# A decoder kernel whose constants and first transfers become operations of its graph, with causal maxima taken as negated minima

## The chip, the cores and the metric

The kernel runs on one core of a Trainium2 chip as one program. The metric is the device time of one execution in microseconds (us). The core has a TensorE (PE: matmuls, with weight loads listed apart as PEld), VectorE (DVE), ScalarE (ACT), GpSimd (POOL) and SyncE (SP), which here only issues transfers. Each engine works through its own stream of instructions in order, and waits on semaphores where it needs what another engine or a transfer made.

## What is computed

The reference is a decoder of four layers on `x` of 4 batches x 256 tokens x 128 features, in float32, with a context `ctx_768` of 4 x 512 x 96 and a mask on the context. Every stage adds to `x`:

```python
x = x + _L0_attn_ref(_layernorm(x), W, b)                    # one head of 128
x = x + _L0_xattn_ref(_layernorm(x), ctx_768, Wq, ..., q_down, q_up, ..., Wk_ipa, Wv_ipa)
...
x = x + _L2_attn_ref(_layernorm(x), Q, K, V, O)              # 16 heads of 64, causal
...
x = x + _L3_attn_ref(_layernorm(x), Wq, Wk, Wv)              # one head of 64, causal
x = x + _L3_xattn_ref(_layernorm(x), ctx_768, ...)
x = x + _L3_ffn_ref(_layernorm(x), ...)                      # 6 layers of local attention and a gated FFN
```

Two pieces matter for the change. In the first cross attention each of the four weights gets a low-rank addition, `W + down @ up * (alpha / 32)`, and the last 4 of the 512 context tokens are image tokens with weights of their own. In the two causal attentions the scores of later tokens are masked, then comes a softmax: maximum of a row, exponential of the difference, sum, division.

## The kernel before, in words

The kernel keeps `x` in four tiles, one for each batch, of 128 partitions x 2 x 128. It is written as a graph: each `op` names an entry of the table `NET` (or `LOCAL` for the last stage) with its engine, an estimated duration and a due time, and lists the buffers that it reads and writes. `Flow.order` (a list scheduler that runs when the kernel is built) sorts all operations of all stages: among the operations that could start first on an engine it takes the one that is due first, and it hands out buffers of an arena (`TILES` says how many of a kind there are). The stages are interleaved by batch in the order of `ORDER`. So what stands next to what on an engine comes from the due times. Where the scheduler sees TensorE wait, it puts filler transposes of the identity matrix in front (`keep`, L412, of tile `ident`): work without a use. In the program of before, TensorE starts with 34 such transposes (`WARM`), and 284 more stand at other places.

What the scheduler does not order in before is the set-up. `Decoder.prepare` (L82 to L130) and `Net.prepare` (L1055 to L1073) and `Net.run` (L1709 to L1723) issue it ahead of the graph:

- POOL makes the identity (`masks.py`), `neghalf`, `ones`, the float32 causal mask (L108, L112), three bfloat16 masks (L126, L128), zeroed tiles for later stages (L1062 to L1072: four of 256 columns, two of 1040, two of 576, and two of 65 ones) and the `pick` tile of the third cross attention (L1712, L1720).
- SP issues the four loads of `x` (L94) and two of the mask (L1715); ACT issues `cols` (the biases and scales by column), `rows` (six bias rows on all partitions) and four context tiles `ctxT` (L82, L97, L100).

Only then comes the graph. Its first operations are, for batch 0 of the first attention: layer norm (`n_stats` on DVE, L440 and L441; `n_eps` on DVE, L445; `n_root`, a power of -0.5, on POOL, L446; `n_scale` on DVE, L456), a turn on TensorE and its copy on ACT (L412, L417), then `h_qk`, `h_v`, `h_scores`, the softmax and `h_weigh`. Its weight `a0_w` is fetched by SP (L426) as an operation of the graph. The first cross attention needs `low_rank` (L819 to L865): eight fetches (for q, k, v and o one of `up`, 32 x 1024, and one of `down`, at most 32 x 128), four scalings by alpha / 32 (`l_scale`, L832), products (`l_mm`) and additions to the weights (`l_add`, L850, L863). Then `image_keys` fetches two weights into the same kind of buffer (`x4`, four of them) and multiplies them with the image tokens: 16 matmuls with only 16 columns each (`i_kv`). A transfer on SP waits for the eighth transfer ahead of it to have landed, and for its buffer to be free.

A causal maximum is one DVE instruction for each block of scores, which adds the mask, writes the sum and keeps the row's maximum; a second instruction for each pair of blocks turns the sign (L548, L777), because the exponential on ACT (L557, L781) takes the negated maximum as its bias:

```python
nc.vector.tensor_tensor_reduce(
    cols(lo, hi), ps2.t[:, lo:hi], d.causal[:, t, : hi - lo], 1.0, -3.0e38, ALU.add, ALU.max,
    one(nmx, t),
)
...
nc.vector.tensor_scalar_mul(nmx.t[:, 2 * e : 2 * e + 2], nmx.t[:, 2 * e : 2 * e + 2], -1.0)
```

The second layer's causal attention has 16 heads in pairs: 4 batches x 8 pairs x 2 heads gives 64 such `c_max` operations, with 2 blocks each. The last layer's has one head: 4 `h_max`.

Of the kernel before, what the change touches and what calls it, by code (L numbers as in the profile page):

```python
# [30 lines left out]
P = 128  # L31
# [17 lines left out]
    ("x0_qal", 1), ("x0_kal", 1), ("x0_val", 1), ("x0_oal", 1), ("desc", 8),  # L49
# [17 lines left out]
class Decoder:  # L67
# [17 lines left out]
    def prepare(self):  # L85
# [3 lines left out]
        self.cols = c.tile([P, NCOL], F32, tag="cols", name="cols")  # L89
        self.rows = self.early.tile([P, NROW], F32, tag="rows", name="rows")  # L90
        self.x = []
        for b in range(B):
            xb = c.tile([P, 2, D], F32, tag=f"x{b}", name=f"x{b}")
            nc.sync.dma_start(out=xb, in_=self.a["x"][b].rearrange("(t p) d -> p t d", p=P))  # L94
            self.x.append(xb)
        self.load(self.cols, "cols", nc.scalar)
        nc.scalar.dma_start(out=self.rows, in_=self.a["rows"].partition_broadcast(P))  # L97
        self.ctxT = self.early.tile([CD, B, NCTX], F32, tag="ctxT", name="ctxT")
        for b in range(B):
            nc.scalar.dma_start(out=self.ctxT[:, b, :], in_=self.a["ctxT"][b])  # L100
# [4 lines left out]

        def mask(name, keeps):
            m = self.early.tile([P, 2, S], F32, tag=name, name=name)
            nc.gpsimd.memset(m, 0.0)  # L108
            for t in range(2):
                for base, q, k in keeps(t):  # L110

                    nc.gpsimd.affine_select(  # L112
                        out=m[:, t, :], in_=m[:, t, :], compare_op=ALU.is_ge, fill=NEG,
                        base=base + q * t * P, pattern=[[k, S]], channel_multiplier=q,
                    )
            return m

        self.causal = mask("causal", lambda t: [(0, 1, -1)])

        self.ident16 = self.early.tile([P, P], BF16, tag="ident16", name="ident16")  # L120
        nc.vector.tensor_copy(self.ident16, self.ident)
        self.causal16 = self.early.tile([P, P], BF16, tag="causal16", name="causal16")
        self.band16 = self.early.tile([P, 2 * P], BF16, tag="band16", name="band16")
        for m, lo, k, q in ((self.causal16, 0, -1, 1), (self.band16, 0, -1, 1), (self.band16, P, 1, -1)):
            m = m[:, lo : lo + P]
            nc.gpsimd.memset(m, 0.0)  # L126

            nc.gpsimd.affine_select(  # L128
                out=m, in_=m, compare_op=ALU.is_ge, fill=-(2.0**100), base=0, pattern=[[k, P]],
                channel_multiplier=q,  # L130
            )
# [11 lines left out]
class Flow:  # L143
# [22 lines left out]
    SETTLED = 9.0  # L166
# [179 lines left out]
class Net:  # L346
# [72 lines left out]
    def fetch(self, kind, *parts):  # L419
# [3 lines left out]
        def dma():  # L423
            for name, lo, hi, rows, view in parts:
                out = w.t[rows if isinstance(rows, slice) else slice(rows), lo:hi]
                self.nc.sync.dma_start(out=out if view is None else view(out), in_=self.a[name])  # L426

        self.op("fetch", dma, [], [w])
# [63 lines left out]
    def biased(self, b, row, reads=()):  # L492
# [3 lines left out]
            x, x, row()[:, None, :].to_broadcast([P, 2, D])), [self.x[b], *reads], [self.x[b]])  # L496


    def one_head(self, b, w, rows, scale, biased, causal):
# [40 lines left out]
        def most():  # L540
            if causal:
                for t in range(2):
                    cut = slice(t * S, t * S + nk[t])
                    nc.vector.tensor_tensor_reduce(
                        pr.t[:, cut], sc.t[:, cut], d.causal[:, t, : nk[t]], 1.0, -3.0e38, ALU.add, ALU.max,
                        sums.t[:, t : t + 1],
                    )
                nc.vector.tensor_scalar_mul(nmx.t[:, :2], sums.t[:, :2], -1.0)  # L548
# [5 lines left out]
        def exps():  # L554
            for t in range(2):
# [3 lines left out]
                    accum_out=sums.t[:, 2 + t : 3 + t],  # L559
# [3 lines left out]
        self.op("h_max", most, [sc], [nmx, pr] if causal else [nmx], [sums, pr])  # L563
# [28 lines left out]
    def pair_weights(self, names, rows):  # L592
        view = lambda x: x.rearrange("p (g m) -> p g m", m=D)
        return {
            m: self.fetch("w4", (name, 0, 1024, rows if m in "kv" else P, view if m == "o" else None))
            for m, name in zip("qkvo", names)
# [35 lines left out]
    def cross_wide(self, stage, w, bias, image=None):  # L632
# [4 lines left out]
        for b in range(B):  # L637
# [3 lines left out]
            v, vmade, vt = self.pair_values(b, w, lambda c, b=b: d.ctxT[:, b, c * P : (c + 1) * P], [], 4)  # L641
# [14 lines left out]
    def cross_pair(self, b, g, w, xT, v, vmade, vt, oT, n, image):  # L656
# [3 lines left out]
        self.op("p_k", lambda: self.mm(pk.t[:, :n], w["k"].t[:CD, cut], d.ctxT[:, b, :n]), [w["k"]], [pk], [kT])  # L660
# [83 lines left out]
    def causal_pair(self, b, g, w, xT, v, vmade, vt, oT):  # L744
# [21 lines left out]
        for e in range(2):  # L766
# [4 lines left out]
            def masked(ps2=ps2, cols=cols, one=one, e=e):  # L771
                for t, lo, hi in tiles:
                    nc.vector.tensor_tensor_reduce(
                        cols(lo, hi), ps2.t[:, lo:hi], d.causal[:, t, : hi - lo], 1.0, -3.0e38, ALU.add, ALU.max,
                        one(nmx, t),
                    )
                nc.vector.tensor_scalar_mul(nmx.t[:, 2 * e : 2 * e + 2], nmx.t[:, 2 * e : 2 * e + 2], -1.0)  # L777

            def exps(cols=cols, one=one):
                for t, lo, hi in tiles:  # L780
                    nc.scalar.activation(  # L781
                        cols(lo, hi), cols(lo, hi), AF.Exp, bias=one(nmx, t), accum_out=one(sums, t)
# [6 lines left out]
            self.op("c_max", masked, [ps2], [prob], [p, nmx])  # L789
# [29 lines left out]
    def low_rank(self, w):  # L819

        nc, d = self.nc, self.d
        parts = {}
        for i, (m, rows) in enumerate((("q", D), ("k", CD), ("v", CD), ("o", RANK))):

            r = slice(RANK * i, RANK * (i + 1))
            low, high = ("down", "up") if m != "o" else ("up", "down")
            n = rows if m != "o" else D
            big = self.fetch("x4", (f"x0_{m}{high}", 0, 1024, r, None))
            small = self.fetch("e2", (f"x0_{m}{low}", 0, n, r, None))

            def scale(m=m, small=small, n=n, r=r):
                nc.vector.tensor_scalar(  # L832
                    small.t[r, :n], small.t[r, :n], d.col(f"x0_{m}al")[r], 1.0 / RANK, ALU.mult, ALU.mult,
                )

            self.op("l_scale", scale, [small], [small])
# [1872 lines left out]
```

## Time and profile before

| quantity | value |
|---|---|
| median of 3 runs | 2117.17 us (2116.97 to 2117.47) |
| the profiled execution's own time | 2120.44 us |
| its span, first to last instruction | 2118.5 us |
| mean granted TensorE clock | 0.986 |
| TensorE busy | 2050.2 us, 97% of the span |
| VectorE busy | 1638.8 us, 77% |
| ScalarE busy | 1179.3 us, 56% |
| GpSimd busy | 993.1 us, 47% |
| moved by DMA | 71.21 MB, mean 34 GB/s |

The profile page gives busy times, a chain of work that ended last, groups of instructions and DMA issues. The trace behind it can also be asked for a stretch of time: instructions in order, what each engine waited for, busy time and granted clock. "L412" is a line of the kernel. A line such as `PE bank L412 <- DVE arena L456: 8.5, 4, 4.4` says that TensorE, on its instruction of L412, was idle for 8.5 us in 4 waits, of which the longest was 4.4 us, and that an instruction of L456 on DVE ended them. TensorE's busy time includes the fillers, and a matmul counts as busy at half clock too.

### The profile page before, as it was taken

The page shows a single profiled execution, that of the slowest core. Times are in us where ns is not written, and L with a number is a line of the kernel's source. Part 1 is how long each engine was busy: PE and PEld are TensorE (multiplying, and loading weights), DVE is VectorE, ACT ScalarE, POOL GpSimd, SP SyncE. Part 2 cuts the span into 40 slices and gives each one's busy share as a digit, 9 for nine tenths or more (in the row PEclk, how much of TensorE's full clock was granted, in tenths as well). Part 3 has the DMA queues.
Part 4 walks back from the last instruction along what each step waited for, and adds up shares of the span by engine and source line. Part 5 has one row for each costly group of instructions (what it writes and reads, how often), then busy time and mean ns, then how long its engine had stood idle before and what let it go on. Part 6 is the DMA issues. An engine that isn't in the chain of part 4 may idle for free.

```text
span 2118.5 us, 59911 instructions
## 1 busy us (share of the span) xinstructions
PE 2050.2 (97%) x24498; PEld 1373.6 (65%) x24499; DVE 1638.8 (77%) x4352; ACT 1179.3 (56%) x2668; POOL 993.1 (47%) x1155
## 2 busy tenths in 40 slices
PE   8999999999999998899999999999999999999998
PEld 6666675776675666666665666666656666666666
DVE  4767777788787668988887688789788797797882
ACT  2654727344536677566565565556556465556553
POOL 3334415231312245445364357557567465575660
PEclk8999999999999999999999999999999999999999
DMA  5000020111020000100000102112121021211101
GB/s 155 1 1 2 1 70 1 32 40 55 2 76 2 9 2 5 56 3 1 1 1 1 51 13 70 42 31 74 42 72 52 25 70 42 71 46 42 29 23 32
DMA packets 33425, 71.21 MB, mean 34 GB/s; under 512 B 5688, under 2 KB 17984, under 8 KB 33152
## 3 DMA queue, kind: packets, MB, share of 16 engines
q1 hardware_dynamic: 20320, 50.29, 8.0%
q10 hardware_dynamic: 12832, 17.09, 2.5%
q8 instruction: 194, 3.18, 0.6%
q14 instruction: 79, 0.65, 0.1%
HBM read 41.68 MB, written 0.52 MB: 20 GB/s over the span
## 4 chain that ended last, share of the span: by engine, by line
PE 68%; DVE 22%; POOL 5%; issue 3%; ACT 2%; DMA 1%; POOLq 0%; SPq 0%; ACTq 0%; DVEq 0%
PE bank L409 39%; PE bank L1828 17%; PE bank L412 9%; PE bank L2044 2%; DVE arena L1982 2%; DVE arena L1992 2%; DVE arena L1997 2%; POOL arena L2034 2%; DVE arena L1603 1%; POOL arena L1996 1%; POOL arena L2077 1%; PE bank L2118 1%; DVE arena L2085 1%; DVE arena L417 1%; DVE arena L2087 1%
## 5 line engine op out<-in xcount | busy, mean ns | idle before, releaser
L409 PE MATMUL bank<-arena 128*64 128x256 f32 (+11 forms) x6824 | 857.5, 393 | 10.5 <-ACT arena L1525 3.6
L409 PEld LDWEIGHTS bank<-arena 128*128 128x128 f32 (+4 forms) x6824 | 532.6, 165 | 276.8 <-issue 100.0
L1828 PE MATMUL bank<-arena 64*64 64x32 f32 (+3 forms) x13584 | 651.7, 251 | 6.4 <-issue 2.6
L1828 PEld LDWEIGHTS bank<-arena 64*64 64x64 f32 (+2 forms) x13584 | 387.4, 127 | 209.3 <-issue 115.9
L417 ACT COPY arena<-bank 128x512 f32<-128x512 f32 (+4 forms) x586 | 269.6, 489 | 286.1 <-PE bank L409 199.9
L1996 POOL TENSOR_TENSOR arena<-arena 128x1024 f32<-128x1024 f32 x96 | 226.7, 2364 | 124.1 <-PE bank L1828 63.4
L691 POOL TENSOR_SCALAR arena<-arena 128x508 f32<-128x508 f32 (+1 forms) x256 | 176.8, 697 | 209.2 <-DVE arena L688 184.1
L412 PEld LDWEIGHTS bank<-ident,arena 128*128 128x128 f32 x1757 | 196.6, 141 | 116.2 <-issue 47.3
L412 PE MATMUL bank<-ident,arena 128*128 128x128 f32 x1757 | 253.5, 280 | 18.3 <-DVE arena L456 8.5
L686 ACT ACTIVATE arena<-bank,arena 128x508 f32<-128x508 f32 (+1 forms) x256 | 175.3, 691 | 78.6 <-DVE arena L684 36.6
L2034 POOL TENSOR_TENSOR arena<-arena 128x1024 f32<-128x1024 f32 x96 | 180.9, 1905 | 71.8 <-DVE arena L2018 71.8
L1990 ACT ACTIVATE arena<-bank 128x512 f32<-128x512 f32 x192 | 113.9, 601 | 133.2 <-PE bank L1828 105.7
L684 DVE TENSOR_REDUCE arena<-bank 128x1 f32<-128x508 f32 (+1 forms) x256 | 164.2, 676 | 18.6 <-PE bank L409 18.4
L1002 ACT ACTIVATE arena<-bank 128x512 f32<-128x512 f32 (+1 forms) x256 | 124.6, 582 | 63.9 <-PE bank L409 62.4
L417 DVE COPY arena<-bank 128x512 f32<-128x512 f32 (+1 forms) x196 | 125.8, 667 | 42.9 <-PE bank L412 27.7
L1992 DVE TENSOR_TENSOR arena<-bank,arena 128x512 f32<-128x512 f32 x192 | 127.5, 683 | 38.0 <-ACT arena L1990 36.4
L2077 POOL TENSOR_TENSOR arena<-arena 128x1024 f32<-128x1024 f32 x48 | 91.4, 1904 | 108.5 <-ACT arena L2050 62.7
L1982 DVE TENSOR_TENSOR arena<-bank,arena 128x256 f32<-128x256 f32 x384 | 138.4, 411 | 3.1 <-ACT arena L1990 2.7
L979 DVE TENSOR_REDUCE arena<-bank 128x1 f32<-128x512 f32 (+2 forms) x256 | 116.7, 513 | 21.5 <-PE bank L409 21.1
L2050 ACT COPY arena<-bank 128x512 f32<-128x512 f32 x192 | 103.3, 601 | 28.8 <-PE bank L2044 28.7
L1997 DVE TENSOR_REDUCE arena<-arena 128x16 f32<-128x1024 f32 x96 | 114.3, 1201 | 0.0
L2044 PEld LDWEIGHTS bank<-ident,arena 128*128 128x128 f32 x768 | 87.0, 142 | 42.0 <-POOL arena L2034 21.8
(230 smaller groups left out, 2460.7 us busy)
## 6 DMA issues: line engine op xcount, KB each, us to landing
arena<-arena SPq DMA_DIRECT2D x48, 384.0 KB, 3.9
arena<-in_f_w SPq DMA_DIRECT2D x24, 512.0 KB, 3.5
arena<-in_f_wqkv ACTq DMA_DIRECT2D x18, 512.0 KB, 7.0
arena<-arena SPq DMA_DIRECT2D x48, 128.0 KB, 2.3
arena<-in_f_wo ACTq DMA_DIRECT2D x6, 512.0 KB, 4.0
arena<-in_f_w ACTq DMA_DIRECT2D x6, 341.0 KB, 3.9
arena<-in_f_w ACTq DMA_DIRECT2D x6, 192.0 KB, 6.2
arena<-in_x_wq SPq DMA_DIRECT2D x2, 512.0 KB
```

Of the source, the lines that this page charges most:

```text
L409: self.nc.tensor.matmul(out, lhsT, rhs, start=start, stop=stop)
L412: self.nc.tensor.transpose(out, in_, self.d.ident)
L417: return self.op(name, lambda: copy(out(), in_()), reads, writes, holds)
L684: self.op("p_max", lambda ps=ps, one=one: nc.vector.tensor_reduce(one(nmx), ps.t[:, :n], AX.X, ALU.max, negate=True), [ps], [most], [nmx])
L686: self.op("p_exp", lambda ps=ps, one=one, cols=cols: nc.scalar.activation(cols(), ps.t[:, :n], AF.Exp, bias=one(nmx), accum_out=one(sums)) ...
L691: nc.gpsimd.tensor_scalar(cols(), cols(), one(sums), 1.0, ALU.mult, ALU.mult)
L1828: self.nc.tensor.matmul(out, lhsT, rhs, start=start, stop=stop)
L1982: nc.vector.tensor_mul(heads(tmp.t[:, cut])[:, :, lo : lo + 32], heads(ps.t)[:, :, 32 - lo : 64 - lo], spread(1, lo, lo + 32),)
L1992: op("cosine", lambda cut=cut, ps=ps: nc.vector.tensor_mul(heads(out.t[:, cut]), heads(ps.t), spread(0, 0, 64)), [ps, w["tab"]], [out])
L1996: op("rotary", lambda: nc.gpsimd.tensor_add(out.t, out.t, tmp.t), [out, tmp], [out])
L1997: op("norms", lambda: nc.vector.tensor_reduce(ss.t[:, at : at + 16], heads(sq.t), AX.X, ALU.add), [sq], [ss])
L2034: nc.gpsimd.tensor_mul(heads(out.t), heads(out.t), rs.t[:, at : at + 16, None].to_broadcast([P, 16, 64]))
```

## The change

The first transfers and the constants become operations of the graph with names, durations and due times of their own (`load_*`, `k_*`); only the identity, `neghalf`, `ones` and the load of `cols` stay ahead of it. All other loads are issued by SP, in the order of their due times; `rows` and `ctxT` leave ACT's queue. The eight low-rank fetches become two, `x0_ups` (128 x 1024) and `x0_downs` (128 x 128), with one scaling for all four. `WARM` falls from 34 to 20. In the causal maxima, the scale of the masked sum is -1.0 and the reduction a minimum, so that the result is the negated maximum; the instruction that turned the sign goes, and the exponential gets the scale -1.0. All due times of `NET` and `LOCAL` are set anew, most by a few units.

```diff
-        self.load(self.cols, "cols", nc.scalar)
-        nc.scalar.dma_start(out=self.rows, in_=self.a["rows"].partition_broadcast(P))
...
-        for b in range(B):
-            nc.scalar.dma_start(out=self.ctxT[:, b, :], in_=self.a["ctxT"][b])
...
+    def load_context(self, b):
+        self.nc.sync.dma_start(out=self.ctxT[:, b, :], in_=self.a["ctxT"][b])
...
                     nc.vector.tensor_tensor_reduce(
-                        cols(lo, hi), ps2.t[:, lo:hi], d.causal[:, t, : hi - lo], 1.0, -3.0e38, ALU.add, ALU.max,
+                        cols(lo, hi), ps2.t[:, lo:hi], d.causal[:, t, : hi - lo], -1.0, 3.0e38, ALU.add, ALU.min,
                         one(nmx, t),
                     )
-                nc.vector.tensor_scalar_mul(nmx.t[:, 2 * e : 2 * e + 2], nmx.t[:, 2 * e : 2 * e + 2], -1.0)
...
-                        cols(lo, hi), cols(lo, hi), AF.Exp, bias=one(nmx, t), accum_out=one(sums, t)
+                        cols(lo, hi), cols(lo, hi), AF.Exp, bias=one(nmx, t), scale=-1.0, accum_out=one(sums, t)
...
+        big = self.fetch("x4", ("x0_ups", 0, 1024, P, None), name="load_ups")
+        small = self.fetch("h", ("x0_downs", 0, D, P, None), name="load_low")
+        self.op("l_scale", lambda: nc.vector.tensor_scalar(
+            small.t[:, :D], small.t[:, :D], d.col("x0_al"), 1.0 / RANK, ALU.mult, ALU.mult), [small], [small])
...
+        begun = Buffer()
+        for b in range(B):
+            self.op("load_x", lambda b=b: d.load_x(b), [], [self.x[b], begun])
+            self.op("load_ctx" if b else "load_ctx0", lambda b=b: d.load_context(b), [], [self.context[b]])
+        self.op("load_rows", d.load_rows, [], [self.rows])
+        self.op("k_causal", d.fill_causal, [begun], [self.causal])
+        self.op("k_ident", lambda: nc.vector.tensor_copy(d.ident16, d.ident), [begun], [self.masks])
+        self.op("k_masks", d.fill_masks, [begun], [self.masks])
...
+        self.op("k_pads", empty, [begun], [b for bufs in pads.values() for b in bufs])
+        self.op("k_values", values, [begun], [self.fixed("vs", self.vss) for _ in self.vss])
+        self.op("k_image", image, [begun], [self.fixed("vb", self.vbs) for _ in self.vbs])
+        self.op("k_pick", pick, [begun], [self.pick])
+        self.op("load_mask", mask, [], [self.pick])
...
+    "load_a": ("SP", 0.8, -900.0),
+    "load_x": ("SP", 0.55, -800.0),
+    "load_low": ("SP", 0.3, -700.0),
+    "load_ups": ("SP", 2.05, -690.0),
+    "load_wk": ("SP", 1.55, -600.0),
+    "load_ctx0": ("SP", 0.8, -540.0),
+    "load_wv": ("SP", 1.55, -500.0),
+    "load_wq": ("SP", 2.05, -400.0),
+    "load_ctx": ("SP", 0.8, -300.0),
+    "load_rows": ("SP", 1.55, -250.0),
+    "load_image": ("SP", 1.55, -200.0),
+    "load_wo": ("SP", 2.05, -150.0),
+    "load_mask": ("SP", 0.9, 30.0),
+    "k_causal": ("POOL", 1.4, 43.74),
+    "k_ident": ("DVE", 0.2, -2.50),
+    "k_masks": ("POOL", 1.7, 7.01),
+    "k_pads": ("POOL", 1.3, -0.06),
+    "k_values": ("POOL", 2.4, 1.19),
+    "k_image": ("POOL", 1.3, 2.10),
+    "k_pick": ("POOL", 3.1, 37.01),
...
-WARM = 34
+WARM = 20
```

The order that the scheduler makes of it can be read off the built programs, instruction by instruction, without any time. On SP the loads stand as in the table above: `a0_w`, the four of `x`, `x0_downs`, `x0_ups`, the weight of k, the first context tile, the weights of v and q, three context tiles, `rows`, the two image weights, the weight of o, the mask. On POOL the first `n_root` stands right behind the identity, ahead of all zeroed tiles, masks and `pick`. On TensorE the 14,099 instructions other than fillers are the same in both programs, and only their places differ, in these stretches (times are those of the profile before): the start up to 81.3 us; small swaps between 169 and 370 us and between 697 and 719 us; 1131 to 1142 us; 1234 to 1354 us, where the last stage begins; and 2002 to 2083 us, before its end. Fillers: 318 before (34 at the start, 45 more in its first 27 us, 18 between 1284 and 1292 us, 8 at 2078 us), 269 after (20 at the start, none until 441 us, 36 between 1270 and 1287 us, none at 2078 us); the others stand where they stood.

## The prediction

> **What bounds the kernel now.** I read the page first (busy times, chain), then TensorE's waits, then the first 50 us instruction by instruction, since most of the change lies there.
>
> ```profile
> PE 2050.2 (97%) x24498; PEld 1373.6 (65%) x24499; DVE 1638.8 (77%) x4352; ACT 1179.3 (56%) x2668; POOL 993.1 (47%) x1155
> PE 68%; DVE 22%; POOL 5%; issue 3%; ACT 2%; DMA 1%; POOLq 0%; SPq 0%; ACTq 0%; DVEq 0%
> ```
>
> TensorE is busy 97% of the span and makes 68% of the chain. So a microsecond counts only where TensorE waits, runs fillers, or runs at half clock. The waits of the first 30 us:
>
> ```profile
> PE bank L412 <- DVE arena L456: 2.9, 2, 2.5
> PE bank L409 <- DVE arena L832: 2.3, 2, 1.4
> PE bank L412 <- POOL ident masks.py:199: 1.6, 1, 1.6
> PE bank L409 <- ACT arena L417: 0.5, 1, 0.5
> ```
>
> What ends them is in the timeline, from layer norm 0 to the low-rank products:
>
> ```profile
> 4.48 4.02 DVE L445 TENSOR_SCALAR arena<-arena 128x2 f32<-128x2 f32 x1
> ...
> 4.86 1.89 POOL L1067 MEMSET arena<- 128x1040 f32 x2
> ...
> 7.93 0.55 POOL L1712 MEMSET pick<- 128x512 bf16 x1
> ...
> 8.58 0.72 POOL L446 TENSOR_TENSOR arena<-arena,neghalf 128x2 f32<-128x2 f32 x1
> ...
> 9.34 1.34 DVE L456 TENSOR_SCALAR arena<-x,arena 128x128 f32<-128x128 f32 x2 [0.78 <-POOL arena L446]
> ...
> 19.70 0.86 DVE L832 TENSOR_SCALAR arena<-arena,cols 32x128 f32<-32x128 f32 x3 [3.28 <-DMA arena<-in_x_qdown]
> ```
>
> Two delays are to be seen. `n_eps` takes 4.02 us, though its like takes 0.14 at 26.49: it ends at 8.50, when POOL's unbroken run of memsets ends (8.48). And the small `qdown`, last in SP's queue, lands at 19.68, so that `l_mm` starts at 20.03. The third loss is the clock, in the table of stretches (columns: time, PE, PEld, DVE, ACT, POOL, clock, DMA share, GB/s):
>
> ```profile
> 27.15:81.30 54.15, 54.15 (x272) 34.15 (x274) 32.81 (x96) 28.42 (x70) 17.92 (x52) 0.91 0.14 50
> 28.00:40.00 12.00, 12.00 (x50) 9.59 (x49) 3.30 (x10) 1.39 (x4) 2.18 (x8) 0.57 0.56 197
> ```
>
> TensorE is granted 0.57 between 28 and 40 us, that is half from 29.6 to 39.85, although it counts as busy: it runs 16-column products there.
>
> **The start, part by part.** The built programs have the same work on TensorE in the same order from 81.3 us on (but for the stretches below), so I compare the time from the first `h_qk` (11.53) to that point: 69.8 us. In it: waits 1.42 + 0.85 = 2.3; 45 fillers at about 0.12 = 5.4; half clock 10.24 x 0.5 = 5.1 and, from 12.5 to 16.0 over some 2.5 us of work, 1.2. Proper work: 69.8 - 2.3 - 5.4 - 6.3 = **55.8 us**. Now the same four terms after.
>
> *When `h_qk` starts.* `a0_w` (192 KB) is ahead of `x0` on SP, one issue of 0.5 us: statistics begin at 4.0 instead of 3.54. They take 0.94 to `n_eps`, this 0.17 (POOL is idle now), `n_root` 0.72, with gaps 5.95. Then `n_scale` meets the moved memsets. Row: at 9.34 two scales took 1.34 beside POOL's selects of 0.63, one in each gap between two of them, which wait for each other. In the new order the zeroed tiles run without a wait for 1.01 + 0.98 us, then comes a 65-column memset that waits for the one ahead: first gap 8.0, second 9.1. With the 0.85 from scale to `h_qk` as before: **10.0**. Bounds: no blocking, 7.2; blocked to the selects of `k_masks`, 11.6. The Trainium skill, page "SBUF — State Buffer", section "SBUF: two separate sides", speaks against this cost: the pair of ports that DVE and GpSimd share is locked for one instruction, so an instruction would wait for the memset under way only. By it `n_eps` would have waited 0.33 us, where the row shows 4.02; by the page `h_qk` would start near 7.6, by the row at 10.0.
>
> *Waits of TensorE after that.* Loads: between 2 and 18 us before, DMA moved 263 GB/s on average, most of it from SP alone. Summed in the new order from 2 us: weight of k 1.76 MB, 8.7 us; of v 2.35 MB, 10.9; of q 2.87 MB, 12.9; second image weight 4.64 MB, 19.6. `l_scale` and the first `l_mm` need 1.36 MB, 7.2. None is late for its first use (`l_mm` near 11, `i_kv` near 22). On DVE the six `l_add` at 0.6 stand in one row with `h_qkout` (0.9) and `h_max` (0.6): 5.1 us from 11.2 on, so the values, which need the last `l_add` of v, start near 16 to 17. TensorE has about 12 us of work from 10.0 to `i_kv`; I take waits of **3 us** (bounds 1 and 6). Queued behind an `l_add` that waits for a weight would be `h_max` and `h_recip`; the sums above leave 2 to 3 us.
>
> *Clock.* 20 starting transposes end near 5.8 instead of 7.5, then TensorE idles until 9: I expect half clock from about 9 to 12.5 or 16 and again for one record of 3.41 us around `i_kv` (its 32 passes take 0.107 each at full, 0.213 at half clock). **4.5 us** lost (bounds 1.5 and 10). The Trainium skill, page "TensorE: Matmul & The Clock Gate", section "What's actually happening", speaks against taking fillers out: an idle window of about 3.4 us halves the clock. The records here have that length too, but the half clock at 29.6 came while TensorE was fed: being fed alone did not keep it.
>
> Sum: 10.0 + 55.8 + 3 + 4.5 = 73.3 against 81.3: **-8.0 us** (bounds 65.5, -15.8; 83.4, +2.1). The 18 transfers, at 0.3 to 0.5 us of issue each, are SP's alone now; SP waits for the eighth before, with over 1 MB under way. ACT loses five issues and is free for its table at 1.3 instead of 8.56; that was hidden already.
>
> **Causal maxima.** 64 + 4 instructions go, of the group
>
> ```profile
> L777 DVE TENSOR_SCALAR arena<-arena x64: 168/169/1161, 661.7 to 916.0; 128x2 f32<-128x2 f32 x64
> ```
>
> whose mean is 0.216 us: 13.9 us of DVE. The number of other instructions stays, so the minimum and the scale of -1 cost what the maximum (0.28 and 0.41) and the exponential (0.40) cost. On the path: between 661 and 925 us TensorE waited 4.1 us in 9 waits for the shares behind this chain, each shorter by 0.2, so **-2.0**. Bounds: all of it on the path, -14.8; nothing, and a clock record of 3.41 us more by a shifted phase, +1.7. Its cover is TensorE's own work; where DVE is fullest,
>
> ```profile
> 795.00:901.00 106.00, 93.86 (x622) 67.15 (x620) 96.87 (x356) 65.60 (x210) 50.13 (x75) 0.95 0.10 31
> ```
>
> half of the 64 stand, and 12 us of TensorE's idle time, mostly behind the latent softmax and not behind `c_max`: what is late next.
>
> **Later orders.** From 1234 to 1354 us other attention heads go first and the first projections of the last stage later; 36 fillers replace 18: +18 x 0.11 = 2.0 if all are on the path, nothing if they fill waits that are there anyway (5.8 us). I take **+1.0**; bounds -5.8 (waits gone) and +5.6 (36 at half clock less 18). Before the end 8 fillers go and the order differs: **-0.5**; bounds -3.2 and +3.2 (the waits in that stretch).
>
> **Sum.** -8.0 - 2.0 + 1.0 - 0.5 = -9.5. Span 2118.5 - 9.5 = 2109.0; with the 1.9 around it 2110.9. The profiled execution is 3.3 above the median, so the median is 2117.2 - 9.5 = **2107.7 us**.
>
> **Rivals.** (1) *The ports and the clock eat the start.* For: `n_eps` at 4.02 us; half clock at 29.6 despite fillers. Against: gaps between dependent POOL instructions did let DVE in. `h_qk` at 11.6 and 10 us of clock: the start gives 0.9, the sum -2.4, 2114.8. (2) *Loads are late, so that the new order does not do what it says.* If SP alone moved the 155 GB/s of the first slice, the image weights land at 32 us and TensorE waits 10 us near 22: +0.5, 2117.7. Against: 245 to 317 GB/s between 10 and 18 us. (3) *Slower: the entry of the last stage.* With its projections behind the other heads, TensorE runs out of work while the first unit goes from scale (1267.8) to share (1292.4). TensorE waits 5.8 us in all of 1229 to 1355; should all 24.5 us of that chain lie bare, that is +18.7 and the sum +8.2, 2125.4. It decides from 14 us extra on. For: the 26 fillers in one place. Against: most heads only change places. (4) *Better:* free ports, full clock, and the rest as forecast: -17.3, 2099.9.
>
> **Chances.** Forecast 0.62 (2102 to 2113), (1) 0.16, (2) 0.06, (3) 0.08, (4) 0.08. The range, 8 in 10: 2097 to 2119, from a little under (4), for waits that also go in the last stage, to a little past (1) and (2). A difference of 0.2%, 4.2 us, is about what a measurement of this kernel can tell from none: faster by more (below 2112.9) 0.72: forecast 0.58, (4) 0.08, part of (1); within it 0.18; slower 0.10: (3) and the tails.
>
> **What would show it.** Right: `n_eps` near 0.2 us, first `h_qk` near 10, the 200th matmul (81.3 before) near 73, no `c_max` sign instruction. Wrong: `n_scale` over 4 us; TensorE waiting for an image weight or an `l_add`; granted clock below 0.9 between 10 and 50 us; waits over 10 us between 1234 and 1354.

## The result, and the profile after

| | before | after |
|---|---|---|
| median | 2117.32 us (2116.97 to 2118.49, 4 runs) | 2101.35 us (2096.44 to 2105.97, 4 runs) |
| ratio | 1 | 0.992, 95% interval 0.9897 to 0.9944 |
| span of the profiled execution | 2118.5 us | 2104.0 us |
| DVE busy | 1638.8 us | 1624.8 us |

The change makes the kernel 16.0 us faster (0.8%), inside the range of the prediction (2097 to 2119) and 6.4 us below its number. The four runs after fall into two pairs, 2096.4 and 2097.0 us at a granted clock of 0.993 and 0.994, 2105.7 and 2106.0 us at 0.986 and 0.989, and the first profile is that of the run of 2105.7 us.

Busy times and chain of the page after:

```profile
PE 2039.5 (97%) x24449; PEld 1364.9 (65%) x24450; DVE 1624.8 (77%) x4281; ACT 1178.2 (56%) x2668; POOL 991.5 (47%) x1155
PE 70%; DVE 20%; POOL 5%; issue 3%; ACT 2%; DMA 0%; POOLq 0%; ACTq 0%; SPq 0%; DVEq 0%
```

The bound is the same; DVE lost 14.0 us (64 + 4 signs and three scalings of the low-rank factors). The timeline of the start (start, duration, then the instruction):

```profile
4.86 0.17 DVE L446 TENSOR_SCALAR arena<-arena 128x2 f32<-128x2 f32 x1
...
5.18 0.71 POOL L447 TENSOR_TENSOR arena<-arena,neghalf 128x2 f32<-128x2 f32 x1 [3.65 <-DVE ident L1066]
...
5.85 1.21 POOL L1073 MEMSET arena<- 128x256 f32 x4
5.93 0.62 DVE L457 TENSOR_SCALAR arena<-x,arena 128x128 f32<-128x128 f32 x2 [0.78 <-POOL arena L447]
...
7.44 1.13 PE L410 MATMUL bank<-arena 128*128 128x256 f32 x4 [0.46 <-ACT arena L418]
...
9.56 1.23 PE L410 MATMUL bank<-arena 32*96 32x512 f32 x4 [0.99 <-DVE arena L521]
```

`n_eps` (L446) takes 0.17 us, the scales (L457) slip in between memsets, the first `h_qk` (L410) starts at 7.44 instead of 11.53, and `l_mm` (32 rows) at 9.56 instead of 20.03: `x0_ups` has landed at 9.43. (The row puts the wait of 0.99 us down to L521, which ended at 9.49; in four other profiles the same wait is put down to the transfer of `x0_ups`.) TensorE's waits between 6 and 45 us were

```profile
PE bank L410 <- DVE arena L521: 1.0, 1, 1.0
PE bank L413 <- DVE arena L457: 0.5, 1, 0.5
PE bank L410 <- ACT arena L418: 0.5, 1, 0.5
```

and the stretches (columns as in the prediction: time, five engines, clock, DMA share, GB/s) show the time from `h_qk` to the 200th matmul, and the two stretches of it in which the granted clock is 0.50. The profile lists such stretches in pieces of 3.41 us; each piece is called a record of half clock here, and costs 1.7 us where TensorE is busy throughout:

```profile
7.44:66.69 59.25, 58.26 (x309) 36.12 (x310) 40.15 (x119) 30.87 (x78) 27.57 (x73) 0.91 0.41 116
9.22:16.05 6.83, 6.49 (x34) 5.24 (x35) 2.64 (x5) 1.02 (x4) 6.23 (x16) 0.50 1.04 241
26.29:29.70 3.41, 3.41 (x5) 1.25 (x5) 2.42 (x7) 0.00 (x0) 0.81 (x2) 0.50 1.01 380
```

To see where the time went I set the same matmul of both programs (fillers not counted) side by side. In the two profiles it comes earlier after the change by

| matmul of before at | 81.3 us | 751 | 1002 | 1058 | 1448 | 2094 | end |
|---|---|---|---|---|---|---|---|
| earlier by, us | 14.7 | 15.0 | 19.1 | 20.7 | 15.6 | 14.8 | 14.5 |

So the start gives 14.7 (the 200th matmul is not the same one in the two orders; from 85 us on, where it is, 14.0), the causal attention 4.1 (751 to 1002), a record of half clock at 1022.9 that does not come back 1.6; the entry of the last stage takes 5.1 back and the end 1.1.

**Theory.** (1) The start gains by the low-rank factors, which no longer land last; POOL's constants matter less. (2) The sign of the maxima lay on the path, for more than its own duration. (3) What is given back at the entry is the new due times'; the 9 us between runs are the clock's. The rivals are told with each run.

### The profile page after: what moved, and what is told of

Read it like the earlier page. It is cut to its first block, busy times and chain, and to the rows that moved or that the text cites. A ratio compares the mean times of both kernels' runs of the same rounds, so it can differ in the third digit from the quotient of the medians.

```text
span 2104.0 us, 59729 instructions
## 1 busy us (share of the span) xinstructions
PE 2039.5 (97%) x24449; PEld 1364.9 (65%) x24450; DVE 1624.8 (77%) x4281; ACT 1178.2 (56%) x2668; POOL 991.5 (47%) x1155
## 4 chain that ended last, share of the span: by engine, by line
PE 70%; DVE 20%; POOL 5%; issue 3%; ACT 2%; DMA 0%; POOLq 0%; ACTq 0%; SPq 0%; DVEq 0%
PE bank L410 40%; PE bank L1844 17%; PE bank L413 9%; PE bank L2060 3%; DVE arena L1998 2%; DVE arena L2013 2%; DVE arena L2008 2%; POOL arena L2050 2%; DVE arena L1637 1%; POOL arena L2012 1%; DVE arena L2101 1%; PE bank L2134 1%; DVE arena L2103 1%; POOL arena L2093 1%; DVE arena L2033 1%
## 5 line engine op out<-in xcount | busy, mean ns | idle before, releaser
L410 PE MATMUL bank<-arena 128*64 128x256 f32 (+11 forms) x6824 | 857.0, 395 | 7.6 <-ACT arena L1559 3.6
L410 PEld LDWEIGHTS bank<-arena 128*128 128x128 f32 (+4 forms) x6824 | 533.3, 166 | 269.2 <-issue 95.9
L418 ACT COPY arena<-bank 128x256 f32<-128x256 f32 (+3 forms) x586 | 270.3, 489 | 272.3 <-PE bank L410 184.5
L413 PE MATMUL bank<-ident,arena 128*128 128x128 f32 x1757 | 253.7, 280 | 15.0 <-DVE arena L457 6.8
L2060 PE MATMUL bank<-ident,arena 128*128 128x128 f32 x768 | 102.1, 279 | 15.9 <-POOL arena L2050 15.8
```

The source lines that it names most:

```text
L410: self.nc.tensor.matmul(out, lhsT, rhs, start=start, stop=stop)
L413: self.nc.tensor.transpose(out, in_, self.d.ident)
L418: return self.op(name, lambda: copy(out(), in_()), reads, writes, holds)
L2060: nc.tensor.transpose(ps.t[:, i * P : (i + 1) * P], out.t[:, (g + i) * P : (g + i + 1) * P], d.ident)
```

## The experiments

All were run beside the kernel before on the same chip (52 runs of it in all, median 2117.8, 2111.0 to 2123.1 us). Single executions of one program differ by up to 10 us here, so besides medians I compare the place of the same matmul in the profiles.

### The maxima alone, and everything but the maxima

`b_min` is the kernel before with

```diff
-   ..., 1.0, -3.0e38, ALU.add, ALU.max, one(nmx, t),
-   nc.vector.tensor_scalar_mul(nmx.t[:, 2 * e : 2 * e + 2], nmx.t[:, 2 * e : 2 * e + 2], -1.0)
+   ..., -1.0, 3.0e38, ALU.add, ALU.min, one(nmx, t),
...
-   AF.Exp, bias=one(nmx, t), accum_out=one(sums, t)
+   AF.Exp, bias=one(nmx, t), scale=-1.0, accum_out=one(sums, t)
```

and the same in `h_max` and `h_exp`; `a_max` is the changed kernel with the opposite edit.

> The kernel before with the causal maxima alone changed (negated minima, no sign instruction); every operation stands in the same order as before. Theory A (the sign stood on the path of the shares in the second layer's causal attention): the stretch 661 to 925 us is 2 to 6 us shorter, the whole 2111 to 2115 us; DVE is busy 13.9 us less. Rival R (what the second layer gained in the changed kernel came from records of half clock that fell on other places, not from the sign): the whole 2115.5 to 2119 us, and the shift in that stretch comes in steps of about 1.7 us, each at a record of half clock.

> The changed kernel with the causal maxima of before put back (maximum, then the sign), in the order of the changed kernel. Theory A: 2 to 6 us slower than the changed kernel, 2103 to 2107 us beside its median of 2101.4. Rival R: no difference but that of the clock, 2099 to 2103 us. Under both the start stays as in the changed kernel: first h_qk at 7.4 us, the 200th matmul at 66 to 67 us.

Measured: `b_min` 2115.89 us (2111.05 to 2119.84, 12 runs), ratio to before 0.9986, interval 0.9977 to 0.9995, some 3 us. `a_max` 2105.45 us (2103.50 to 2111.76, 6 runs), 3.8 us above the control of the next set. In the profiles, `b_min` gains 5.3 us on before between the matmuls of 751 and 1002 us. TensorE's waits for the shares behind the maxima (the division that ends the softmax, on POOL; line, engine it waited for, us in total, times, longest), first before, then `b_min`, `a_max` and the changed kernel:

```profile
PE bank L412 <- POOL arena L787: 4.1, 9, 1.2
```

```profile
PE bank L412 <- POOL arena L785: 2.3, 8, 0.4
```

```profile
PE bank L413 <- POOL arena L791: 4.1, 9, 1.2
```

```profile
PE bank L413 <- POOL arena L789: 1.4, 5, 0.4
```

With the sign 4.1 us in 9 waits in either order, without it 2.3 or 1.4. That is 1.8 us of the 5.3 that `b_min` gains. The rest is two records of half clock that before has and `b_min` has not, 1.7 us each. The one at 893.2 belongs to the sign: it follows the wait of 1.2 us, which ends at 893.0. `a_max` has the same (a record at 885.6 behind a wait of 1.2 us that ends at 884.8), and in the twelve profiles without the sign the wait at this place is 0.4 us and no record follows. The one at 862.5 does not belong to it. It follows a wait for the exponential of another softmax, which `b_min` has as well, without the record (before, then `b_min`):

```profile
PE bank L412 <- ACT arena L1524: 2.0, 1, 2.0
```

```profile
PE bank L412 <- ACT arena L1522: 2.0, 1, 2.0
```

Five other profiles without the sign have a record at this place (`a_again` at 842.5), so that `b_min` is without it by luck. That leaves 1.8 + 1.7 = 3.5 us for the sign, near the 3 us between the medians and the 3.8 of `a_max`. So both halves of what I had set against each other are true: the sign was on the path (theory A), and about half of its price came through the clock (rival R). The whole of `b_min`, 2115.9 us, lies in R's range. The changed kernel's first profile gains its 4.1 us without the clock: between the two matmuls it has as much half clock as before (10.2 us, at other places), and TensorE's idle time falls from 13.8 to 11.1 us.

### Due times

`a_due` is the changed kernel with the due times of before for all old operations (tables as in before, new rows kept):

```diff
-NET_PACE = 1.175628
+NET_PACE = 1.177894
...
-LOCAL_PACE = 1.081089
+LOCAL_PACE = 1.098019
```

> The changed kernel with the due times of before for all operations that both have (NET, LOCAL and their paces); the new operations keep theirs. Theory E (the new due times cost 3 to 5 us at the entry of the last stage): TensorE waits less between 1220 and 1340 us and the whole is 2096 to 2099 us beside 2101.4 for the changed kernel. Rival N (the new due times are worth something elsewhere, in the second layer and at the start, and the loss at the entry is the clock's): 2101 to 2108 us.

Measured: 2104.19 us (2100.25 to 2107.93, 6 runs), in rival N's range. Theory E falls: the old due times don't bring back 3 to 5 us. Between the matmuls of 1058 and 1448 us the profile of `a_due` loses nothing against before (its lead goes from 13.95 to 14.05), but it has 6.8 us of half clock there and before has 17.1; at equal clock it would lose 5 us, like the changed kernel. TensorE's order there is nearly that of the changed kernel in spite of the old due times: of 4304 records of matmuls 50 differ from it and 362 from before. So the entry's order does not come from the old operations' due times. What is left is what the new and the dropped operations do to the scheduler; no run shows that by itself. At the start `a_due` is only 7.8 us ahead of before at the 200th matmul, with 17.1 us of half clock, so what the new due times are worth there is not settled.

### POOL's constants

`a_pool` issues the memsets ahead of the graph again; the operations stay in the graph, empty, so that nothing else moves. `a_free` goes the other way: the zeroed tiles come behind the masks and the pick tile.

```diff
-        self.op("k_pads", empty, [begun], ...
+        d.fill_causal(); nc.vector.tensor_copy(d.ident16, d.ident); d.fill_masks()
+        empty(); values(); image()
+        self.op("k_pads", lambda: None, [begun], ...
```

```diff
-        self.op("k_pick", pick, [begun], [self.pick])
+        self.op("k_pick", lambda: [pick(), empty(), values(), image()], [begun], [self.pick])
```

> The changed kernel with the causal mask, the three bfloat16 masks and the zeroed tiles issued ahead of the graph again, as before (the pick tile stays in the graph); the order of all other engines and queues is that of the changed kernel. Theory Q (the queue on POOL: n_root stands behind the memsets, whatever n_eps does): n_root starts at 8 to 8.6 us, the first h_qk at 10.5 to 11, and some 3 us of it are left at the 200th matmul (69 to 70 us): 2104 to 2105 us. Rival P (the ports: DVE is locked out for the whole run of memsets that don't wait for each other): n_eps takes 3 to 4 us again, and more than n_root is late. Rival L (the loads set the start): the first h_qk is late by 3 us, but l_mm and the products behind it are not, and the 200th matmul stays at 66 to 67.5 us. If n_eps takes under 0.6 us beside the same run of memsets, P falls, and only Q or L is left.

> The changed kernel with the zeroed tiles issued on POOL behind the three masks and the pick tile, whose instructions wait for each other; the order of everything else is kept. Theory P (a run of POOL's memsets that do not wait for each other keeps DVE's scale out until its end in most executions: 1.97 us in five profiles, 0.56 us in two): n_scale takes 0.3 to 0.7 us, the first h_qk starts at 7.3 to 7.6 us in every execution; l_mm still waits for x0_ups until 9.4 to 11.1 us, so the whole gains under 1 us. Rival: n_scale takes 1.9 us beside the selects too, so the run is not what keeps it out.

Measured: `a_pool` 2103.12 us (2100.69 to 2104.72, 5 runs), `a_free` 2103.55 us (2099.75 to 2110.26, 6 runs), both within the spread of the control. Timeline of `a_pool`:

```profile
4.94 3.08 DVE L446 TENSOR_SCALAR arena<-arena 128x2 f32<-128x2 f32 x1
...
8.11 0.72 POOL L447 TENSOR_TENSOR arena<-arena,neghalf 128x2 f32<-128x2 f32 x1
...
10.59 0.79 PE L410 MATMUL bank<-arena 128*128 128x256 f32 x1 [0.46 <-ACT arena L418]
```

`n_eps` is blocked again (P), but `n_root` stands behind the memsets on POOL anyway (Q): it starts at 8.11, so `n_eps` cost nothing of its own. `h_qk` is 3.15 us later than in the changed kernel's profile, the 200th matmul 1.4, at 68.1 (between Q and L). How much of the 3.15 the loads cover is not settled by that, because the clocks differ: behind `h_qk`, `a_pool` ran some 6.6 us at half clock (3.2 of them up to 13.8 us, where its records begin; its matmuls of 128x256 start 0.43 us apart there and 0.22 later), the first profile 10.2 us. Reckoned at equal clock the 200th matmul is some 3 us later. In the medians `a_pool` is 1.4 us above the control. Now the same place in the second control, `a_third`, and in `a_free`:

```profile
5.96 2.04 DVE L457 TENSOR_SCALAR arena<-x,arena 128x128 f32<-128x128 f32 x2 [0.78 <-POOL arena L447]
...
7.91 0.24 POOL L1079 MEMSET arena<- 128x65 f32 x1
```

```profile
6.01 0.60 DVE L457 TENSOR_SCALAR arena<-x,arena 128x128 f32<-128x128 f32 x2 [0.78 <-POOL arena L447]
...
7.46 0.92 PE L410 MATMUL bank<-arena 128*128 128x256 f32 x3 [0.46 <-ACT arena L418]
```

In `a_third` the two scales end at 7.93 and 8.00, when the first memset that waits for another (L1079, 7.91) ends the run. In the ten profiles with the memsets in that place, the scale took 1.97 us in seven (`h_qk` near 8.9) and 0.56 in three (7.4 to 7.6). Beside the selects of `a_free`, which wait for each other, it takes 0.35. P holds, with an exception that I could not foretell: the scale starts 0.08 us after the first memset in both kinds of execution. On the whole time it has no effect that can be measured. In the four profiles in which `h_qk` starts at 7.4 to 7.6 TensorE then waits 1.0 to 2.6 us ahead of `l_mm`, until `x0_ups` has landed; where the scale was blocked and `x0_downs` stands in its place, that wait is 1.1 us in `a_warm` and nothing in the other five. There the transfer, not POOL, sets when `l_mm` starts.

### The low-rank factors

`a_low` puts the load of `x0_downs` behind the image weights.

```diff
-    "load_low": ("SP", 0.3, -700.0),
+    "load_low": ("SP", 0.3, -160.0),
```

> The changed kernel with the load of the low-rank factors x0_downs put behind the image weights on SP, so that it lands late as qdown did before; the scheduler then puts h_v, h_turn and h_weigh and 45 fillers ahead of l_mm, as in the kernel before. Theory D (the late low-rank factor was the largest part of what the start lost): l_mm starts at 22 to 25 us, the 200th matmul comes at 75 to 81 us, the whole is 7 to 12 us slower than the changed kernel. Rival (the other work covers it): 200th matmul before 71 us, at most 3 us slower.

Measured: 2113.47 us (2110.11 to 2119.41, 9 runs), 11.8 us above the control: theory D. The 200th matmul comes at 80.0. `l_mm` starts at 29.9, later than expected. A wait and the clock of `a_low`:

```profile
PE bank L410 <- DMA arena<-in_x_wki: 3.2, 1, 3.2
```

```profile
22.20:35.90 13.70, 12.94 (x71) 12.58 (x72) 7.77 (x26) 1.27 (x4) 3.82 (x10) 0.50 0.67 227
```

With the factors late the scheduler puts 45 fillers and `i_kv` ahead of `l_mm`; before, there were 45 fillers too, 21 ahead of `l_mm` and 24 behind its first products, and `i_kv` came later. 13.7 us at half clock follow. One transfer of 64 KB, in another place of SP's queue, is worth most of the start, with the order that the scheduler makes of it. The edit goes further than the kernel before did: the factors land at 24.4 us here, at 19.7 to 20.2 before and at 6.5 in the control. And it does not tell the early place from the merging: eight small factors in an early place were not run.

### Transfers of x behind, more fillers at the start, and the control

`a_ups` issues `x` of batches 1 to 3 behind `x0_ups`; `a_warm` has `WARM = 34`; `a_again` and `a_third` are the changed kernel.

```diff
-        self.op("load_x", lambda b=b: d.load_x(b), ...
+        self.op("load_x", lambda b=b: None if b else d.load_x(b), ...
...
+            if name == "x0_ups":
+                for b in range(1, B):
+                    self.d.load_x(b)
```

```diff
-WARM = 20
+WARM = 34
```

> The changed kernel itself once more, as the control of its neighbours. Theory V (the same program takes 5 us more or less at the start from execution to execution: x0_ups lands between 9.4 and 11.1 us and the records of half clock fall on other work): median 2100 to 2104 us, the 200th matmul somewhere between 66 and 73 us, the second layer as in the first profile. Rival (the first profile showed the normal start, the slower start belonged to the other kernel): the 200th matmul at 66 to 67.5 us again.

> The changed kernel with the loads of x for batches 1 to 3 issued behind x0_downs and x0_ups on SP; every other order is kept. Theory L (l_mm waits for x0_ups, which waits for its turn on SP): x0_ups lands 1 to 1.5 us earlier than in the control, TensorE waits under 0.5 us for it, the 200th matmul is 1 to 2 us earlier and the whole 1 to 2 us faster. Rival W (the transfers share the DMA engines, so the order of issue within 1.5 us matters little): x0_ups lands within 0.5 us of the control, no difference.

> The changed kernel with 34 starting transposes in place of 20. Theory C (the half clock of 9 to 16 us follows TensorE's idle time from 5.8 to 7.4 us): the starting transposes end at 7.3 to 7.5 us, the first h_qk is late by at most 0.4 us, no record of half clock before 16 us, and the 200th matmul is 2 to 3 us earlier than with 20 of them in a like start. Rival K (the half clock comes from the waits and small products behind it): records of half clock between 9 and 16 us as in the control, and no gain.

Measured: `a_again` 2101.70 us (2096.18 to 2103.76, 5 runs), 200th matmul at 64.3; `a_ups` 2101.75 us (2097.16 to 2112.08, 6 runs), at 66.0; `a_warm` 2104.09 us (2099.05 to 2108.51, 6 runs), at 67.1. Theory V's spread is there, and wider than it said. In six profiles whose start is that of the changed kernel the 200th matmul comes at 64.3, 66.5, 66.7, 67.2, 69.1 and 71.7 us: `x0_ups` lands between 9.4 and 11.1, and one to four records of half clock fall on the first 36 us. The worst is `a_max`:

```profile
PE bank L410 <- DMA arena<-in_x_ups: 2.6, 1, 2.6
```

In `a_ups` TensorE does not wait for `x0_ups`, but in its profile the scale was blocked, and then the controls don't wait either, so that nothing is left to see (neither L nor W is shown). `a_warm` has no record of half clock before 26.8 us, where all eleven profiles with 20 transposes are at half clock somewhere between 7.8 and 13.8 us (C is right on the cause, as far as one profile shows). The 200th matmul is no earlier than in the controls: TensorE waits 1.1 us for `x0_ups` and 1.3 us for an addition instead. C is wrong on the gain.

### The clock in the last stage

In `a_fill` TensorE gets fillers where it waits anyway.

```diff
+FILLED = {0: 10, 32: 10, 64: 10, 96: 10, 128: 10, 160: 10}
+FILLED_FLIP = {1632: 34, 1920: 13}
...
     def transpose(self, out, in_):
+        for _ in range(FILLED_FLIP.get(self.flips, 0)):
+            self.nc.tensor.transpose(out, self.d.ident, self.d.ident)
+        self.flips += 1
...
                     def turn(ps=ps, out=out, g=g):
+                        self.net.turns += 1
+                        for _ in range(FILLED.get(self.net.turns - 1, 0)):
+                            nc.tensor.transpose(ps.t[:, :P], d.ident, d.ident)
```

> The changed kernel once more as control. Theory G: median 2099 to 2104 us; records of half clock in the last stage only where the 1.40 us wait ahead of a layer's first turn lies wholly in one window of 3.41 us, none where a window's border cuts it into parts under about 0.9 us. Rival H: a record behind a wait that is cut, or none behind one that lies wholly in a window.

> The changed kernel with fillers in TensorE's known waits: 10 ahead of the first turn of each of the six layers of the last stage (waits of 1.4 to 1.6 us), 34 ahead of the turn that waits 4.4 us near 1095, 13 ahead of the one that waits 1.95 us near 1262; nothing else differs. Theory G (a wait that fills over some 40% of one 3.41 us window of the clock makes the next window half clock, 1.7 us; the 1.40 us wait that comes back once per layer does or does not, by where the window's border falls, and so the same program takes 2096 or 2106 us): no record of half clock behind the six turns, one or two fewer at 1095 and 1262, granted clock 0.993 or more, median 3 to 7 us below the control, the slow executions gone. Rival H (the clock goes by something else than TensorE's idle time, or the fillers push real work later): records at the same period of 140 us as in the first profile, or a median not below the control.

> The kernel of a_fill once more, because its first four runs (median 2098.6 us) and the control's (2101.6 us) overlap. Theory G: median 2096 to 2100 us, no record of half clock behind the first turns of the six layers. Rival H: median 2101 us or more, so that a_fill's first median was chance.

Measured: `a_third` 2101.63 us (2097.33 to 2103.91, 6 runs), `a_fill` 2098.61 us (2096.40 to 2101.40, 4 runs), `a_fill_b` 2099.09 us (2096.86 to 2101.79, 5 runs, on another chip than the first two). Stretch 1355 to 2000 us in `a_third`, then in `a_fill`:

```profile
1355.00:2000.00 645.00, 623.02 (x11552) 415.95 (x11551) 531.45 (x1097) 367.70 (x622) 402.94 (x223) 0.99 0.17 49
```

```profile
1355.00:2000.00 645.00, 629.24 (x11625) 421.04 (x11624) 534.73 (x1102) 371.24 (x626) 403.36 (x223) 1.00 0.17 49
```

Three records of half clock in the one, none in the other, and none in `a_fill_b` either. The records near 1095 and 1262 us, 6.8 to 13.7 us in the three profiles of the changed kernel, are gone too. The granted clock of the nine runs is 0.990 to 0.993 (0.993 or more was expected). The medians are 3.0 and 2.5 us below the control (3 to 7 were expected). All nine runs with fillers lie between 2096.4 and 2101.8 us (median 2099.1), the fifteen of the changed kernel between 2096.2 and 2106.0 (median 2101.7); seven of the fifteen are slower than the slowest of the nine. But the ratios to before (0.9915 and 0.9920 against 0.9913 to 0.9925) overlap, so the gain of 2 to 3 us is likely and not settled. Both profiles with fillers also have half clock near 1300 us (10.2 and 3.4 us) that the controls lack.

G's rule for the wait was wrong, though. The same 1.40 us wait ahead of a layer's first turn, with the stretches of 3.41 us around it, in the changed kernel:

```profile
1521.33:1524.74 3.41, 2.01 (x123) 1.90 (x116) 3.28 (x10) 1.43 (x3) 2.24 (x2) 1.00 0.53 129
1524.74:1528.15 3.41, 3.41 (x12) 2.29 (x11) 1.27 (x2) 1.37 (x3) 3.41 (x2) 0.50 0.26 69
```

and in `a_third`:

```profile
1518.54:1521.95 3.41, 2.02 (x55) 1.67 (x48) 3.41 (x7) 1.75 (x4) 3.33 (x2) 1.00 0.74 193
1521.95:1525.36 3.41, 3.41 (x16) 2.83 (x15) 0.17 (x1) 0.98 (x2) 3.41 (x3) 1.00 0.01 4
```

In both TensorE is busy 2.0 of 3.41 us and the wait lies wholly in the window; the next window is granted 0.50 in the one and 1.00 in the other. What differs is where in the window the wait ends: 0.28 us ahead of its border in the first, 1.37 in the second. Over the 63 waits of 1.2 to 1.7 us between 1340 and 2000 us in the twelve profiles without these fillers: all 23 that end between 0.53 us ahead of a border and 0.27 behind it are followed by half clock, 9 of 14 that end 0.57 to 0.82 ahead, and none of the 26 others. Behind 2000 us this is not the whole rule: one of three that end near a border is not followed by half clock, and of 15 that end farther from one 8 are, like one of 1.29 us in `a_third` that ends 1.01 us ahead of it:

```profile
2051.01:2054.42 3.41, 2.12 (x145) 2.01 (x141) 1.59 (x3) 2.38 (x6) 1.58 (x1) 1.00 0.49 124
2054.42:2057.83 3.41, 3.41 (x40) 2.00 (x34) 0.00 (x0) 1.48 (x3) 0.32 (x1) 0.50 0.27 73
```

## Why the prediction was right, and where not

The direction, the range and the mechanism (the start gives most, the maxima next, the later orders take a little back) were right; all three sizes were off. Both gains were put too low and the loss too low as well, so that the sum missed the median by 6.4 us and not by more: that part is luck.

**The start: -8.0 forecast, -14.7 in the profile** (six profiles: -9.6 to -17.0). The step that failed is the sum 10.0 + 55.8 + 3 + 4.5. Its terms for the first `h_qk` (7.4 to 9.1 us measured) and for the proper work (53.1 to 53.7) were too large in all six profiles, and the waits came from a transfer that it had too early:

| term, us | forecast | first profile | `a_again` | `a_max` |
|---|---|---|---|---|
| first `h_qk` | 10.0 | 7.4 | 8.9 | 7.5 |
| proper work | 55.8 | 53.2 | 53.4 | 53.6 |
| waits | 3 | 1.0 | 0.3 | 3.8 |
| half clock | 4.5 | 5.1 | 1.7 | 6.8 |
| 200th matmul | 73.3 | 66.7 | 64.3 | 71.7 |

(Proper work is the stretch less the idle time and half of the records; the other rows are read off.) Against the 81.3 us of before, the 14.7 of the first profile are 5.4 of dropped fillers, as forecast, 4.1 by the earlier `h_qk` (1.5 forecast), 2.6 of work (0), 1.3 of waits (-0.7) and 1.2 of half clock (1.8). *`h_qk`:* the first gap, at 8.0, was where I had put it; I then let the second scale wait for a second gap at 9.1, and both went in at the first. Where the scales came through at once (7.4 to 7.6), TensorE waited for `x0_ups` instead, so the earlier `h_qk` is worth less than it looks. The row of 4.02 us, on which I read the blocking, was real and cost nothing, since `n_root` was queued behind the same memsets. *Proper work:* it was a remainder, 69.8 less fillers, waits and clock, and I took it for constant. The products of `l_mm`, before (those for q, k and v, then those for the output weight) and in the first profile:

```profile
20.03:22.52 2.49, 2.49 (x13) 1.47 (x13) 2.00 (x6) 0.00 (x0) 0.00 (x0) 1.00 0.03 7
27.15:29.12 1.97, 1.97 (x16) 1.85 (x16) 1.97 (x5) 0.00 (x0) 1.61 (x3) 1.00 1.00 388
```

```profile
9.56:11.58 2.02, 2.02 (x14) 1.80 (x14) 0.00 (x0) 0.00 (x0) 1.88 (x7) 0.50 1.06 251
13.59:15.61 2.02, 2.02 (x15) 1.80 (x15) 1.28 (x2) 1.02 (x4) 1.84 (x4) 0.50 1.06 247
```

At full clock that is 4.5 us before and 2.0 after. With one factor for all four, the products for the output weight start 0.02 us behind the others and run beside them. This gain of the merged factor, 2.4 us, I had not seen. *Waits:* I had put DVE's row of additions behind `h_max`; TensorE had other work. The loads ran 2 to 4 us later than my sum (`x0_ups` at 9.4 to 11.1 against 7.2). The sum let the transfers land one after the other; by 9.43 us some 1.86 MB had moved since 2 us (7.43 us at 250 GB/s) and not 1.36, so later transfers ran beside it. It cost 1.0, 1.4 and 2.6 us in three profiles of six. *Clock:* 4.5 was near the mean of a quantity that runs from 1.7 to 6.8.

The Trainium skill, page "SBUF — State Buffer", section "SBUF: two separate sides", has the pair of ports that DVE and GpSimd share held for the whole of one instruction, while the other engine is blocked. If the lock changed hands at that instruction's end, as the prediction read it, `h_qk` would have started near 7.6; three of ten profiles agree (7.4 to 7.6), seven do not: there the scale waited through five memsets.

**The maxima: -2.0 forecast, some -3 to -4 found** (-3 between the medians of `b_min` and before, -4.1 in the first profile; 1.7 of the -5.3 in `b_min`'s profile are luck). The term "each shorter by 0.2" gave the right total for `b_min`'s waits (4.1 to 2.3), though most of it lies in few of them (the longest went from 1.2 to 0.4). Missing was the record of half clock behind that wait, 1.7 us. I had put the clock into the bounds with the wrong sign only (+1.7).

**The later orders: +1.0 forecast, about +5 found.** Between the matmuls of 1058 and 1448 us the first profile gives back 5.1, with as much half clock there as before (17.1 us). `a_third` gives back 2.1 and `a_again` 0.8, but with 6.8 us of half clock, which is worth 5.1 us; at equal clock 7.2 and 5.9. TensorE's idle time between these matmuls grew from 13.6 to 16.1, and 18 fillers more are 2.0: that is 4.5 of it. I had let the waits swallow the fillers; both grew. The upper bound (+5.6) was the better number. Before the end -0.5 was forecast; behind 1448 us the lead falls by 1.1 (15.6 to 14.5), with 3.4 us more of half clock up to the matmul of 2094, which is worth 1.7.

**The rivals.** (1) fell: the ports did block in most executions and hardly counted. (2) fell: the image weights landed at 21 to 25 us, not 32. (3) fell: 5 to 7 us at equal clock, not 18.7. (4), 2099.9, is nearest to the median, and for the wrong reason: its ports were free in three profiles of ten, the clock at the start was full in none, and it had no loss of 5 us behind.

## What to carry to other kernels

Look first for the small transfer that stands last in a queue and is needed first: 64 KB in the wrong place, with the order that the scheduler made of it, cost 11.8 us here; constants ahead on POOL cost 1.4 us between medians, which is within the spread. A wait of TensorE is to be priced twice, by its length and by the half clock behind it (1.7 us a window), and fillers inside it can remove the second part only (2.5 to 3 us here, likely and not settled). Where single executions differ by more than the effect sought, compare the same instruction's place in several profiles, and test with an edit that keeps the order of everything else.

## What was not expected of the hardware

- The windows of the clock lie on a grid of 3.413 us in every profile. Up to 2000 us a wait of 1.40 us, 41% of a window, is followed by a window at half clock only if it ends near a border (within 0.82 us ahead of it or 0.27 behind); later ones of 1.3 to 1.7 us also where they end 1.0 to 2.0 ahead. What else decides stays open. The Trainium skill, page "TensorE: Matmul & The Clock Gate", section "What's actually happening", has the free-running window of this length; it asks for an idle window, where these rows show far less to be enough.
- In the last stage the wait comes back after some 137.9 us at full clock and, mostly, after 139.4 to 139.8 where it cost 1.7; 41 windows are 139.95 us. So a layer that was caught is followed by one whose wait ends only some 0.4 us earlier in its window, and three or four layers in a row are caught (records at 1384.8, 1524.7, 1664.7 and 1804.6 in the first profile). This, with the start, fits the 9 us between executions of one program.
- Half clock also came while TensorE was busy throughout: from 26.3 us in the first profile, from 28.8 to 35.6 in `a_max`, around the 16-column products. `a_again`, with the same products, has none there. Why stays open.
- A run of POOL's memsets that do not wait for each other kept DVE's scale out until its end in seven executions of ten, and let it through in 0.56 us in three. What decides it stays open.
